# A scan layer and a routed transformer layer in one kernel: where the first batch's router scores are computed, and how the pools of the two layers are cut

## The chip, the cores and the metric

The kernel runs on one core of one Trainium2 chip. The metric is the time of one execution in microseconds (us) of device time. Three executions of the kernel before took 4037.52, 4037.91 and 4040.02 us; the median is 4037.91 us. One execution was taken by the profiler: it took 4038.12 us and its trace spans 4036.3 us from the first to the last instruction.

## The reference, cut to what matters

x is 16 batches of 1024 tokens of 512 float32 numbers. Layer 0 is a selective scan (16 states per channel) with a residual; layer 1 is a routed transformer layer: a router scores every token, the best 127 tokens of a batch go through attention and a feed-forward network, the others pass.

```python
# layer 0
x = x + s6(layernorm(x), A_log, D, x_proj_w, dt_proj_w, dt_proj_b)
#   s6: delta = softplus(...); h = exp(delta*A)*h + delta*B*u over the tokens; y = sum(h*C) + u*D
# layer 1, on h = layernorm(x) of the result
weights = (h @ router_w)[..., 0] + router_b[0]      # one score per token
topv, topi = top_k(weights, 128); thr = topv[:, -1]
sel_idx = sort(topi[:, :127])
x_sel, pos_sel, w_sel, m_sel = h, positions, weights and mask rows at sel_idx
x1 = x_sel + attention(rmsnorm(x_sel, ln1), m_sel) @ wo
x2 = x1 + gelu(rmsnorm(x1, ln2) @ w1) @ w2
out = put x2 * w_sel at sel_idx, plus h where weight <= thr
x = x + out
```

## The kernel before, in words

**The scan** (`scan_layer`) works through 32 halves: 16 batches, two halves of 512 tokens each. A half is 64 steps g: 16 states n by 4 channel blocks dc of 128 channels. For one step TensorE builds the input db in one of four PSUM banks of 2 KB (`turn`, lines 308 to 321, two steps ahead), ScalarE builds the decay da (`decays`, five steps ahead) and the scaled input v (`scaled`, eight ahead), VectorE does the recurrence in place (`recur`, line 329), GpSimd multiplies two steps' result by C (`weighed`, line 341) and TensorE sums the states into y (`summed`, line 360, six steps behind). SyncE's queue fetches dg twelve steps ahead (`diagonals`, line 283) and ct (`fetch`). While one half runs, the small generators `prep` (softplus and input of the next half) and `stats` (mean and variance of the next batch) are advanced one piece per step by `until(k)`. `finish` (line 249) turns y back and adds it to x1 in device memory by a GpSimd-issued DMA (line 265). The last half has no `prep` and no `stats` beside it.

**The routed layer** (`ffn_layer`) is a software pipeline of periods p of 28 ticks each. In period p these generators are advanced tick by tick, in this order: `feed(p-1)`, `attention(p)`, `keep_others(p)`, `select(p+1)`, `scores(p+2)`. So period -2 has scores(0) alone, period -1 has select(0) and scores(1), period 0 has attention(0), select(1), scores(2), and so on.
- `scores(b)` (lines 618 to 660): for each of 8 chunks of 128 tokens, VectorE takes bn_stats and bn_aggr of x1 and a product with the router's weight row rw, summed (lines 630, 631, 633); then 1/sqrt(variance) and the score of every token; the scores go through a TensorE transpose (652), a DMA to device memory (656) and a DMA that broadcasts them to 128 partitions, w_row (658).
- `select(b)` ranks each token's score against the whole row: three VectorE counts for each chunk (676, 680, 685; the last one needs the triangular matrix `earlier`), the one-hot sel (696), a matmul (710), two gathers by GpSimd (726, 730), and at last the normalized input hnT of the attention.

**Order.** Within each layer's `manual_schedule` block, the instructions of an engine keep the order in which the generators issue them. Instructions outside these blocks, such as the constants and weight loads ahead of the routed layer's loop, are placed by the scheduler: in the trace, VectorE runs line 568 (ahead of the block) after line 630 (inside it).

**Memory.** Pools of SBUF are stacked. The scan's are `s_const` (2 KB and less for each tile), `s_pool` (all large tiles: xt, u, uT, delta, rest, du, dg, v, da, hc, ct, yT) and `s_small`. At the end of `scan_layer` they are given back, and the routed layer's `f_const`, `f_keep`, `f_row`, `f_small` take the same addresses. `f_const` holds the projections wq, wk, wv, wo (1 MB each) and w1, w2 (4 MB each), loaded by twelve DMAs on ScalarE's queue (lines 552, 556, 558).

The loop that sets which generators run:

```python
for p in range(-2, B + 1):
    stages = [stage(b) for stage, b in ((feed, p - 1), (attention, p), (keep_others, p),
              (select, p + 1), (scores, p + 2)) if 0 <= b < B]
    for k in range(PERIOD):
        clock[0] = k
        ...
        for g in list(stages):
            if next(g, "end") == "end": stages.remove(g)
```

Of the kernel before, what the change touches and what calls it, by code (L numbers as in the profile page):

```python
# [19 lines left out]
P = 128  # L20
# [11 lines left out]

@with_exitstack
def scan_layer(ctx, tc, x, x1_dram, a_log, dskip, xpT, dtT, dtb, ident):
# [27 lines left out]
    const = ctx.enter_context(tc.tile_pool(name="s_const", bufs=1))  # L62
    pool = ctx.enter_context(tc.tile_pool(name="s_pool", bufs=2))
    small = ctx.enter_context(tc.tile_pool(name="s_small", bufs=2))
# [24 lines left out]
    eye = const.tile([P, S], F32, tag="eye", name="eye")  # L89
# [3 lines left out]
    skip = const.tile([P, ND, S], F32, tag="skip", name="skip")  # L93
# [155 lines left out]
    def finish(b, half, ys, over):  # L249

        s = f"{b}_{half}"
        turned = over.rearrange("p c (j i r) -> p c j i r", i=NS, r=S)
        yield from until(BEHIND + 1)
        yT = []
        for i in range(NS):
            yT.append(pool.tile([P, LH], F32, tag="yT", bufs=4, name=f"yT_{s}_{i}"))
            nc.scalar.copy(yT[i], ys[i])
        for i in range(NS):
# [7 lines left out]
            x1_dram[b][:, half * TH : (half + 1) * TH, :], over, accum_op=ALU.add  # L266
        )
# [32 lines left out]
    def decays(g):  # L300
        h, n, dc = at(g)
        if dc == 0:
            da_of[h, n] = pool.tile([P, ND, LH], F32, tag="da", bufs=4, name=f"da_{h}_{n}")
        nc.scalar.activation(  # L304
            da_of[h, n][:, dc, :], live[h][1][:, dc, :], AF.Exp, scale=a_sb[:, dc, n : n + 1]
        )
# [27 lines left out]
    def weighed(g):  # L334
# [5 lines left out]
        hc = pool.tile([P, 2, LH], F32, tag="hc", bufs=6, name=f"hc_{h}_{n}_{dc}")  # L340
# [10 lines left out]
    def fetch(h, n):  # L351
        t = pool.tile([P, G, LH], F32, tag="ct", bufs=4, name=f"ct_{h}_{n}")
        nc.sync.dma_start(t, rows_c[h][n : n + G, :].partition_broadcast(P))
        ct_next[h, n] = t
# [28 lines left out]
    with tc.manual_schedule():  # L383
# [10 lines left out]
        for g in range(-AHEAD_D, total + per_half // 2):  # L394
# [4 lines left out]
            if g % per_half == 0 and 0 <= g <= total:  # L399
                h = g // per_half  # L400
                if h + 1 < len(halves):
                    running.append(prep(*halves[h + 1]))
            if 0 <= g + AHEAD_D < total:
                diagonals(g + AHEAD_D)
# [26 lines left out]
            if k >= 0 and k % per_half == per_half - 1 and k < total:  # L431
                h = k // per_half
                running.append(finish(*halves[h], ys_of.pop(h), live.pop(h)[2]))
# [7 lines left out]
def ffn_layer(  # L441
    ctx, tc, x1_dram, mask, pos, router_w, router_b, wq, wk, wv, wo, w1, w2, ln1, ln2, out, ident
# [22 lines left out]
    const = ctx.enter_context(tc.tile_pool(name="f_const", bufs=1))  # L465
    keep = ctx.enter_context(tc.tile_pool(name="f_keep", bufs=2))
    row = ctx.enter_context(tc.tile_pool(name="f_row", bufs=2))
    small = ctx.enter_context(tc.tile_pool(name="f_small", bufs=3))
    dram = ctx.enter_context(tc.tile_pool(name="f_dram", bufs=2, space=DRAM))
# [18 lines left out]
    for q in (0, 2, 4):  # L488
        load(0, q, "x1a")
    rw = const.tile([P, D], F32, tag="rw", name="rw")  # L490
    nc.sync.dma_start(rw, router_w.rearrange("d o -> (o d)").partition_broadcast(P))
    rb = const.tile([P, 1], F32, tag="rb", name="rb")
    nc.sync.dma_start(rb, router_b.partition_broadcast(P))

    gains = const.tile([ND, 2, P], F32, tag="gains", name="gains")
    for i, g in enumerate((ln1, ln2)):
        nc.sync.dma_start(gains[:, i, :], g.rearrange("(c p) -> c p", p=P))
# [10 lines left out]
    )  # L508
    inv = const.tile([P, HH], F32, tag="inv", name="inv")
# [3 lines left out]
    for i in range(HH):  # L513
        nc.vector.memset(inv[:, i : i + 1], float(freq[i]))

    pos_i = const.tile([MB * NT, P], I32, tag="pos_i", name="pos_i")
    for m in range(MB):
        nc.sync.dma_start(
            pos_i[m * NT : (m + 1) * NT, :], pos[m, 0:L].rearrange("(c p) -> c p", p=P)
        )  # L520
    pos_r = const.tile([MB * NT, P], F32, tag="pos_r", name="pos_r")
    nc.vector.tensor_copy(pos_r, pos_i)
    pos_ps = pst.tile([P, 512], F32, tag="tp", name="pos_ps")
    nc.tensor.transpose(pos_ps[:, : MB * NT], pos_r, ident[: MB * NT, : MB * NT])
    pos_f = const.tile([P, MB, NT], F32, tag="pos_f", name="pos_f")
    nc.vector.tensor_copy(pos_f.rearrange("p m c -> p (m c)"), pos_ps[:, : MB * NT])


    POS, WT, TOK, ROW, RSTD, OFF, SIDE = range(7)
    sides = []  # L530
    for i in range(3):
        t = const.tile([P, NT, SIDE], F32, tag=f"side{i}", name=f"side{i}")
        nc.gpsimd.iota(
            t[:, :, TOK], pattern=[[P, NT]], base=0, channel_multiplier=1,
            allow_small_or_imprecise_dtypes=True,
        )
        nc.gpsimd.iota(
            t[:, :, ROW], pattern=[[1, NT]], base=0, channel_multiplier=NT,
            allow_small_or_imprecise_dtypes=True,
        )  # L540
        sides.append(t)

    w_pad = []
    for i in range(2):
        t = const.tile([P, P], F32, tag=f"w_pad{i}", name=f"w_pad{i}")
        nc.vector.memset(t, 0.0)
        w_pad.append(t)

    proj = {}
    for name, wt in (("wq", wq), ("wk", wk), ("wv", wv), ("wo", wo)):  # L550
        proj[name] = const.tile([P, ND, D], F32, tag=name, name=f"{name}_sb")
        nc.scalar.dma_start(proj[name], wt.rearrange("(c p) e -> p c e", p=P))
    w1_sb = const.tile([P, ND, F], F32, tag="w1", name="w1_sb")
    w2_sb = const.tile([P, NF, D], F32, tag="w2", name="w2_sb")
    for c in range(ND):
        nc.scalar.dma_start(w1_sb[:, c, :], w1[c * P : (c + 1) * P, :])
    for c in range(0, NF, ND):
        nc.scalar.dma_start(
            w2_sb[:, c : c + ND, :],
            w2[c * P : (c + ND) * P, :].rearrange("(c p) e -> p c e", p=P),  # L560
        )
    gain = const.tile([P, 2, ND], F32, tag="gain", name="gain")
    for i in range(2):
        g_ps = pst.tile([P, 512], F32, tag="tp", name=f"g_ps{i}")
        nc.tensor.transpose(g_ps[:, :ND], gains[:, i, :], ident[:ND, :ND])
        nc.vector.tensor_copy(gain[:, i, :], g_ps[:, :ND])
    rw_sum = const.tile([P, 1], F32, tag="rw_sum", name="rw_sum")
    nc.vector.tensor_reduce(rw_sum, rw, AX.X, ALU.add)
# [9 lines left out]
    w_row_of, keeping, picked, attended = {}, {}, {}, {}  # L578
# [12 lines left out]
    def taken(ps, name, tag, bufs=1):  # L591
        t = row.tile(list(ps.shape), F32, tag=tag, bufs=bufs, name=name)
# [3 lines left out]
    def gained(ps, i, name, tag):  # L596

        t = row.tile([P, ND, P], F32, tag=tag, bufs=1, name=name)
# [19 lines left out]
    def scores(b):  # L618

        side, wp = sides[b % 3], w_pad[b % 2]  # L620
        w_col = wp[:, :NT]
        st = small.tile([P, NT, nc.vector.BN_STATS_DIM], F32, tag="st", name=f"st_{b}")
        mv = small.tile([P, NT, nc.vector.BN_AGGR_DIM], F32, tag="mv", name=f"mv_{b}")
        xd = small.tile([P, NT], F32, tag="xd", name=f"xd_{b}")
# [410 lines left out]
```

## Time and profile before

| stretch of the profiled execution | us | what |
|---|---|---|
| whole execution / span of its trace | 4038.12 / 4036.3 | |
| 2722.25 to 2807.36 | 85.11 | half 30 of the scan, with the last `prep` beside it |
| 2807.36 to 2882.42 | 75.06 | half 31, the last, with nothing beside it |
| 2882.42 to 2904.00 | 21.58 | last products of GpSimd, `finish`, the DMA that adds y to x1 |
| 2904.00 to 2951.03 | 47.03 | period -2: constants, weights, scores(0) |
| 2951.03 to 2993.64 | 42.61 | period -1: select(0), scores(1) |
| 2993.64 to 3056.92 | 63.28 | period 0 |
| 3056.92 to 3119.03 | 62.11 | period 1; the later ones take about 62 us as well |

The stretches begin and end with VectorE's first or last instruction of the stage. How to read the profile: a timeline row gives start, duration, engine, line, operation, out<-in and count, and in brackets how long the engine had been idle and what ended that. Busy times of VectorE's instructions overlap a little, so a start-to-start distance is shorter than the recorded duration. A window row gives each engine's busy time in a stretch, the clock that TensorE was granted, and the share of time that the 16 DMA engines were busy.

### The profile page before, as it was taken

How to read it: one execution, taken by the hardware profiler on the slowest of the kernel's cores; microseconds unless marked ns; L12 is line 12 of the kernel's file. 1: busy time of each engine (PE TensorE's matmuls, PEld its weight loads, DVE VectorE, ACT ScalarE, POOL GpSimd, SP SyncE). 2: the span in 40 equal slices, each digit the busy share in tenths (PEclk: the TensorE clock that was granted, in tenths of full speed). 3: DMA queues.
4: the chain of work that ended last, by engine and by line, in shares of the span. 5: the costliest groups of instructions: out<-in, count | busy, mean ns of one | idle time of the engine just before them, and what ended most of it. 6: DMA issues, size and time to landing. Idle time of an engine off the chain costs nothing.

```text
span 4036.3 us, 89081 instructions
## 1 busy us (share of the span) xinstructions
PE 3607.3 (89%) x35349; PEld 2272.0 (56%) x35349; DVE 3439.1 (85%) x5142; ACT 3169.2 (79%) x5525; POOL 2716.9 (67%) x1454
## 2 busy tenths in 40 slices
PE   6999999998999999999999999899638999999996
PEld 4666666655666665566666656566324555555453
DVE  5999999999999999999999999999666776867741
ACT  6999999999999999999999999999415455455552
POOL 4899999988999998899999889999600111010110
PEclk8999999999999999999999999999758999999998
DMA  5343433434343343434344343433453434434331
GB/s 152 88 121 82 121 102 103 110 99 122 85 121 95 107 106 106 120 83 121 82 120 111 100 122 86 117 85 104 126 190 106 146 92 154 128 110 150 109 92 33
DMA packets 367466, 444.48 MB, mean 110 GB/s; under 512 B 182381, under 2 KB 252185, under 8 KB 362442
## 3 DMA queue, kind: packets, MB, share of 16 engines
q1 hardware_dynamic: 317080, 371.32, 30.4%
q0 software_dynamic: 40960, 50.55, 6.6%
q10 hardware_dynamic: 9010, 16.91, 1.1%
q8 instruction: 279, 4.57, 0.5%
q14 instruction: 137, 1.12, 0.1%
HBM read 361.36 MB, written 110.66 MB: 117 GB/s over the span
## 4 chain that ended last, share of the span: by engine, by line
PE 44%; DVE 36%; ACT 10%; issue 5%; DMA 3%; POOL 1%; POOLq 0%; DVEq 0%; ACTq 0%; SPq 0%
DVE da L329 19%; PE db L316 13%; PE y L360 8%; PE db L318 6%; PE ff_ps L939 4%; ACT da L304 4%; PE pp L176 3%; ACT v L296 2%; DVE junk L680 2%; DVE junk L676 2%; PE tpy L262 2%; DVE st L630 1%; PE at_ps L896 1%; DVE xw L633 1%; PE tpu L169 1%
## 5 line engine op out<-in xcount | busy, mean ns | idle before, releaser
L341 POOL TENSOR_TENSOR hc<-da,ct 128x1024 f32<-128x1024 f32 x1024 | 2410.5, 2389 | 250.3 <-DVE da L329 193.2
L304 ACT ACTIVATE da<-delta,a_sb 128x512 f32<-128x512 f32 x2048 | 1403.5, 712 | 33.5 <-POOL carry L347 28.5
L316 PE MATMUL db<-dg,du 128*128 128x128 f32 x7168 | 1262.9, 293 | 149.4 <-DVE da L329 130.8
L316 PEld LDWEIGHTS db<-dg,du 128*128 128x128 f32 x7168 | 970.7, 191 | 718.3 <-DVE da L329 542.4
L329 DVE TENSOR_TENSOR_SCAN da<-da,carry,db 128x512 f32<-128x512 f32 x1024 | 1227.7, 1258 | 59.3 <-PE db L318 59.3
L329 DVE TENSOR_TENSOR_SCAN da<-da,db 128x512 f32<-128x512 f32 x1024 | 1175.3, 1197 | 75.1 <-PE db L318 55.3
L318 PE MATMUL db<-ident,v 128*128 128x128 f32 x4608 | 842.1, 274 | 0.0
L296 ACT ACTIVATE v<-du,bT 128x512 f32<-128x512 f32 x1152 | 822.6, 714 | 11.8 <-DVE du L247 6.2
L360 PE MATMUL y<-hc,eye 32*32 32x512 f32 x16384 | 633.0, 606 | 3.2 <-POOL hc L341 2.9
L318 PEld LDWEIGHTS db<-ident,v 128*128 128x128 f32 x4608 | 577.0, 143 | 0.0
L705 POOL PARTITION_ALL_REDUCE thr<-thr_s x16 | 6.2, 385 | 488.0 <-DVE thr_s L704 488.0
L946 POOL DMA_INDIRECT out<-xs,at x16 | 76.0, 4748 | 360.9 <-DVE trig L779 263.0
L939 PE MATMUL ff_ps<-w_sb,gT 128*128 128x512 f32 x512 | 278.3, 663 | 0.0
L914 PE MATMUL up<-w_sb,h2T 128*128 128x512 f32 x512 | 240.5, 598 | 4.0 <-DVE h2T L599 4.0
L360 PEld LDWEIGHTS y<-hc,eye 32*32 32x32 f32 x16384 | 141.0, 103 | 128.9 <-issue 87.2
L208 PE MATMUL z<-xp,dt_sb 97*128 97x512 f32 x256 | 141.6, 636 | 45.1 <-DVE da L329 43.2
L233 POOL TENSOR_TENSOR delta<-delta,rest 128x1024 f32<-128x1024 f32 x64 | 152.0, 2375 | 31.9 <-ACT delta L230 31.9
L593 ACT COPY gT<-tp_g 128x512 f32<-128x512 f32 x64 | 38.2, 596 | 165.6 <-PE tp_g L588 165.6
L914 PEld LDWEIGHTS up<-w_sb,h2T 128*128 128x128 f32 x512 | 92.7, 191 | 100.5 <-issue 92.6
L863 ACT ACTIVATE a<-a,mx 128x127 f32<-128x127 f32 x256 | 98.8, 387 | 54.5 <-DVE mx L861 52.1
L680 DVE TENSOR_SCALAR_CACHE_REDUCE junk<-w_row,side 128x1024 bf16<-128x1024 f32 (+7 forms) x128 | 103.4, 808 | 44.6 <-DMA w_row<-w_dram 44.6
L939 PEld LDWEIGHTS ff_ps<-w_sb,gT 128*128 128x128 f32 x512 | 95.3, 209 | 65.6 <-issue 65.5
(191 smaller groups left out, 3961.2 us busy)
## 6 DMA issues: line engine op xcount, KB each, us to landing
ct<-bc SPq DMA_DIRECT2D x256, 512.0 KB
dg<-field SPq DMA_DIRECT2D x384, 128.0 KB
xt<-in_x SPq DMA_DIRECT2D x32, 1024.0 KB
x<-in_x SPq DMA_DIRECT2D x16, 2048.0 KB
x<-du POOLq DMA_DIRECT2D x32, 1024.0 KB, 8.0
x1a<-x SPq DMA_DIRECT2D x64, 512.0 KB
x1b<-x SPq DMA_DIRECT2D x64, 512.0 KB
out<-x1b SPq DMA_DIRECT2D x64, 512.0 KB
```

Of the source, the lines that this page charges most:

```text
L208: nc.tensor.matmul(z, dt_sb[:, dc * P : (dc + 1) * P], xp, start=True, stop=True)
L233: nc.gpsimd.tensor_tensor(delta[:, dc : dc + 2, :], delta[:, dc : dc + 2, :], rest[:, dc : dc + 2, :], ALU.add)
L296: nc.scalar.activation(v_of[h, n][:, c - m, :], du[:, c, :], AF.Copy, scale=bT[:, c, n : n + 1])
L304: nc.scalar.activation(da_of[h, n][:, dc, :], live[h][1][:, dc, :], AF.Exp, scale=a_sb[:, dc, n : n + 1])
L316: nc.tensor.matmul(out, live[h][2][:, c, ch], dg[:, c, :], start=True, stop=True)
L318: nc.tensor.transpose(out, v[:, c - m, ch], ident)
L329: nc.vector.tensor_tensor_scan(da[:, dc, :], da[:, dc, :], db_of.pop(g), carry[b][:, dc, n : n + 1] if half else 0.0, ALU.mult, ALU.add,)
L341: nc.gpsimd.tensor_tensor(hc, da_of[h, n][:, dc - 1 : dc + 1, :], ct_of[h][:, n % G, :].unsqueeze(1).to_broadcast([P, 2, LH]), ALU.mult,)
L360: nc.tensor.matmul(ys[i][j * S : (j + 1) * S, :], weights(r, j), rows(r, j), start=start, stop=stop, tile_position=(i * S, j * S),)
L680: nc.vector.tensor_scalar(junk[:, lo:], w_row[:, lo:], mine, None, ALU.is_gt, ALU.add, accum_out=cnt[:, 1, c : c + 1],)
L914: nc.tensor.matmul(up, h2T[:, c, :], w1_sb[:, c, f * 512 : (f + 1) * 512], start=(c == 0), stop=(c == ND - 1),)
L939: nc.tensor.matmul(ff_ps, gT[f][:, c, :], w2_sb[:, f * 4 + c, :], start=(f == 0 and c == 0), stop=(f == UP - 1 and c == 3),)
```

## The change

- A class `Router` takes over the router's constants, the side tables, the score buffers and `scores`. It is built ahead of the scan, so its tiles (w_row among them) lie below both layers' pools.
- In the scan's last half a new generator `first_scores` runs where `prep` would. At step 1 it issues the constants' DMAs (rw, rb, two gains, four positions) and loads x1 of batch 0 (four DMAs of 512 KB) into the tile that held xt. At step 8 it prepares the constants. Then for each chunk c a matmul with the identity copies x1 into a PSUM bank at step 9 + 4c, and at step 10 + 4c VectorE does the three score instructions on that bank. At steps 42, 44 and 46 follow 1/sqrt(variance), here as Ln and Exp on ScalarE, the scores, and their way to w_row.
- The routed layer starts with period -1. There scores(1) runs its chunks at ticks 9 to 16 instead of 0 to 5, 13 and 14.
- The scan's pools: da, hc, ct, yT, eye and skip move to a new pool `s_last`, stacked last; the last half's `finish` writes into a da buffer instead of du. The routed layer's pools are stacked as `f_small`, `f_keep`, `f_row`, `f_const` (now without w1, w2), then `f_late` (the tags first written at tick 24 of period -1 or later) and `f_heavy` (w1, w2).
- The projections are loaded on SyncE's queue, alternating with the loads of x1 of batch 1. w1 and w2 are loaded in eight pieces of 1 MB on SyncE's queue at ticks 1 to 8 of period 0. The 16 small writes of `inv` move into select(0).

```diff
+    def scores(self, b, until, slots, chunk, scratch, bank, root, ahead=0):
...
+        for c in range(NT):
+            yield from until(slots[c] - ahead)
+            x1 = chunk(c)
+            yield from until(slots[c])
+            nc.vector.bn_stats(st[:, c, :], x1)
+            nc.vector.bn_aggr(mv[:, c, :], st[:, c, :])
+            nc.vector.scalar_tensor_tensor(
+                scratch(c), x1, 1.0, self.rw, ALU.mult, ALU.mult, accum_out=xd[:, c : c + 1]
+            )
+        yield from until(slots[NT])
...
+            nc.scalar.activation(var, mv[:, :, 1], AF.Ln, bias=self.eps)
+            nc.scalar.activation(rstd, var, AF.Exp, scale=-0.5)
+            yield from until(slots[NT + 1])
+        nc.vector.scalar_tensor_tensor(off, mv[:, :, 0], -1.0, rstd, ALU.mult, ALU.mult)
+
+        nc.vector.tensor_tensor(xd, xd, rstd, ALU.mult)
+        nc.vector.scalar_tensor_tensor(xd, off, self.rw_sum, xd, ALU.mult, ALU.add)
+        nc.vector.tensor_scalar(w_col, xd, self.rb, None, ALU.add)
+        nc.vector.tensor_copy(side[:, :, self.WT], w_col)
+        nc.vector.tensor_copy(side[:, :, self.POS], self.pos_f[:, min(b, self.MB - 1), :])
...
@@ scan_layer
     const = ctx.enter_context(tc.tile_pool(name="s_const", bufs=1))
+    small = ctx.enter_context(tc.tile_pool(name="s_small", bufs=2))
     pool = ctx.enter_context(tc.tile_pool(name="s_pool", bufs=2))
-    small = ctx.enter_context(tc.tile_pool(name="s_small", bufs=2))
+
+    last = ctx.enter_context(tc.tile_pool(name="s_last", bufs=2))
...
+        if over is None:
+            over = last.tile([P, TH, D], F32, tag="da", bufs=4, name="over_last")
...
+    def first_scores():
+
+        yield from until(1)
+        constants = router.constants(bank)
+        next(constants)
+        x1 = pool.tile([P, NT, D], F32, tag="xt", bufs=1, name="x1_early")
+        for q in range(0, NT, 2):
+            nc.sync.dma_start(x1[:, q : q + 2, :], x1_dram[0][:, q : q + 2, :])
+        yield from until(8)
+        _drain(constants)
+        junk = pool.tile([P, TH, D], F32, tag="u", bufs=1, name="junk_early")
+
+        def lifted(c):
+
+            t = bank(f"lift_{c}")
+            nc.tensor.matmul(t, ident, x1[:, c, :], start=True, stop=True)
+            return t
+
+        yield from router.scores(
+            0, until, [10 + 4 * c for c in range(NT)] + [42, 44, 46], lifted,
+            lambda c: junk[:, c % TH, :], bank, False, 1,
+        )
...
                 if h + 1 < len(halves):
                     running.append(prep(*halves[h + 1]))
+                elif h < len(halves):
+                    running.append(first_scores())
...
@@ ffn_layer
-    const = ctx.enter_context(tc.tile_pool(name="f_const", bufs=1))
+    small = ctx.enter_context(tc.tile_pool(name="f_small", bufs=3))
     keep = ctx.enter_context(tc.tile_pool(name="f_keep", bufs=2))
     row = ctx.enter_context(tc.tile_pool(name="f_row", bufs=2))
-    small = ctx.enter_context(tc.tile_pool(name="f_small", bufs=3))
-    dram = ctx.enter_context(tc.tile_pool(name="f_dram", bufs=2, space=DRAM))
+    const = ctx.enter_context(tc.tile_pool(name="f_const", bufs=1))
+
+    late = ctx.enter_context(tc.tile_pool(name="f_late", bufs=2))
+    heavy = ctx.enter_context(tc.tile_pool(name="f_heavy", bufs=1))
...
+    for q, (name, wt) in enumerate((("wq", wq), ("wk", wk), ("wv", wv), ("wo", wo))):
+        if q < 3:
+            load(1, 2 * q, "x1a")
+        nc.sync.dma_start(proj[name], wt.rearrange("(c p) e -> p c e", p=P))
...
+    def load_heavy(i):
+        if i < ND:
+            nc.sync.dma_start(w1_sb[:, i, :], w1[i * P : (i + 1) * P, :])
...
+        first = 9 if b == 1 else 0
...
     with tc.manual_schedule():
-        for p in range(-2, B + 1):
+        for p in range(-1, B + 1):
...
+                if p == 0 and 1 <= k <= ND + NF // ND:
+                    load_heavy(k - 1)
```

## The prediction

> **What bounds the kernel now.** I read the chain that ended last first. Up to 2882 us it alternates between VectorE's recurrences, TensorE and GpSimd; then, for some 70 us, it is a string of waits and transfers (columns: start us, us, what):
>
> ```profile
> 2888.59 7.23 issue
> 2895.84 7.79 DMA x<-du
> 2904.26 13.87 DMA wk_sb<-in_wk
> 2919.10 4.69 DMA pos_i<-in_pos
> ...
> 2928.47 8.90 DMA x1a<-x
> 2937.39 0.74 ACTq L558
> 2938.17 1.28 ACT L640
> 2941.58 4.33 DMA w_dram<-w_t
> 2945.93 4.97 DMA w_row<-w_dram
> 2951.03 1.29 DVE junk L680 x2
> ```
>
> Every engine starts the routed layer only after the scan's last DMA, x<-du, has landed (2904), and select(0)'s first count waits until 2951 for scores(0). Busy times by stretch come second (stretch, length, then PE, PEld, DVE, ACT, POOL busy, clock, DMA share, GB/s):
>
> ```profile
> 2807.36:2882.42 75.06, 73.38 (x914) 47.23 (x914) 75.06 (x65) 58.30 (x95) 75.06 (x36) 1.00 0.26 69
> 2882.42:2904.00 21.58, 10.14 (x78) 4.01 (x76) 0.03 (x1) 4.30 (x8) 7.05 (x4) 0.50 0.28 50
> 2904.00:2951.00 47.00, 1.08 (x4) 0.64 (x4) 14.14 (x65) 1.75 (x3) 0.99 (x8) 0.50 0.96 363
> 2951.00:2993.60 42.60, 12.59 (x49) 10.23 (x50) 30.91 (x120) 9.30 (x20) 2.65 (x3) 0.54 0.39 126
> ```
>
> In the last half VectorE has no idle time at all, so work added there lengthens it. For the 68.6 us behind it (2882.42 to 2951.03) VectorE does only 14.2 us of work. Third, what a VectorE instruction costs beside GpSimd's products, from the groups by line of VectorE (busy us, mean ns):
>
> ```profile
> L138 DVE BATCH_NORM_STATS2 st<-xt 128x6 f32<-128x512 f32 x128 | 86.6, 676 | 3.1 <-DMA xt<-in_x 3.1
> L213 DVE SCALAR_TENSOR_TENSOR rest<-z,delta 128x512 f32<-128x512 f32 x128 | 86.0, 672 | 18.6 <-ACT delta L211 18.5
> L633 DVE SCALAR_TENSOR_TENSOR xw<-x1a,rw 128x512 f32<-128x512 f32 x128 | 84.2, 658 | 0.0
> L146 DVE SCALAR_TENSOR_TENSOR off<-mv,rstd 128x8 f32<-128x8 f32 x16 | 9.1, 570 | 2.1 <-ACT rstd L144 1.9
> ```
>
> The first two run in the scan at the speed of the third, which runs with GpSimd idle. The fourth, 8 elements wide, takes 570 ns where its twin at line 643 takes 174; its two inputs are both SBUF tiles. The timelines around one of them show why (VectorE, then GpSimd):
>
> ```profile
> 2609.67 0.63 DVE L146 SCALAR_TENSOR_TENSOR off<-mv,rstd 128x8 f32<-128x8 f32 x1
> 2610.22 3.43 DVE L329 TENSOR_TENSOR_SCAN da<-da,db 128x512 f32<-128x512 f32 x3
> ```
> ```profile
> 2607.91 2.36 POOL L341 TENSOR_TENSOR hc<-da,ct 128x1024 f32<-128x1024 f32 x1
> 2610.24 2.37 POOL L233 TENSOR_TENSOR delta<-delta,rest 128x1024 f32<-128x1024 f32 x1
> ```
>
> It ends when GpSimd's running product ends.
>
> **The sum.** The profiled execution took 4038.1 us, 0.2 above the median of 4037.9; the sum is made on it.
>
> (a) *scores(0) in the last half.* For eight chunks: bn_stats, bn_aggr and product follow each other every 1.41 us in period -2 (2926.95 to 2928.36): 11.3 us. No row has bn_stats on a PSUM bank; line 213, which reads one, is 14 ns from line 633, which doesn't, so I take the same; bounds 10.5 and, at 0.3 us more for each of 16 reads, 16. Constants: two memsets 0.31, cast 0.2, the round trip by TensorE 0.54 (pos_r's end to pos_f), copies 0.14, the reduction 0.6: 1.9 with the eps. Tail: 1.0 (2939.94 to 2940.95), plus 0.8 for waiting on GpSimd's products (about 0.5 at line 146, a little for the constants). All 15.0 is on the path, since nothing there is idle. And waits can come with it: half 29, of the same kind as half 31 but with `prep` beside it, took 87.15 by VectorE's timeline (2635.10 to 2722.25), 12.1 more, for twelve VectorE instructions of 0.62 start to start, 7.5; 4.6 are waits, most of them of recurrences for db. Here TensorE gets eight matmuls of 512 columns, as from `prep`, but not its 36 transposes; I add 1.0. Together **16.0**; bounds 12.5 (the instructions alone, cheap) and 21.
>
> Hidden beside it: TensorE's eight copies at 0.43 (wq_ps: 1.72 for four), 3.4 us, since weight loads wait for VectorE's banks (32.9 us between 2700 and 2880); 4 us if that cover is gone. ScalarE's Ln and Exp with two table loads of 1.28: it is busy 58.3 of 75.06. GpSimd's six iotas, 0.14 each: with 15 us more for the same 32 products it gets idle time. SyncE issues twelve more DMAs, about 0.37 each (line 486), 4.4 us, and 2 MB at the 0.4 MB/us of period -2 is 5.2: 9.6 us in which dg behind them can be late, against 10 steps of 1.17 between dg's issue and its use. It just fits; a few us if it doesn't. The wait for w_t at step 46 holds the last dg's, with 8 steps in hand.
>
> (b) *The gap.* VectorE's last recurrence is at 2882.4 + 16.0 = 2898.4; call it T. The tiles in `s_pool` and below (by their sizes 112 KB a partition, against 98 for `f_small` to `f_const`) are last read by TensorE's last db, before T. So select(0) may start at T, w_row having been there for 17 steps. **Removed: 68.6.** What is late next is `earlier`: its affine_select (0.29) sits on GpSimd, whose last product runs from T to T + 2.4, and the third count would start at T + 1.3: **+1.4**; bounds 0 and, if GpSimd's queue puts it behind x<-du (`finish` issues that 7.25 after the last product), +9.8. `finish` itself leaves the path: x<-du lands at about T + 18, and `f_late` is first written at T + 35.
>
> Loads: four projections and 1.5 MB of x1 now start at T - 3, 5.5 MB, 14 us, done by T + 11; wq is first read at T + 35. If that cover were gone, 14 us at most.
>
> (c) *Period -1 took 42.6.* Six chunks of scores(1) no longer stand between select's counts: -8.5. Three of them, ticks 9 to 11, now stand ahead of the gathers, beside the 2.2 us for which VectorE waited on line 714: +2.0. The other five and 1.9 us of angles run beside the gathers (7.9 us), and the variance, 9 us behind them, then holds ScalarE's xs by about 0.8; the Sqrt table load (1.28), formerly done in period -2, comes in ahead of it: together +1.8. **-4.7**, bounds -8 (TensorE granted more than 0.54 after a shorter pause) and -2.
>
> (d) *Period 0 and later.* w1 and w2 were loaded in period -2; now 8 MB, 21 us, are issued from tick 1, done by about 25 us into a period of 63; first read at its end. SyncE's x1 loads and stores queue behind them, for chunks needed 30 us later. 0, bounds -1 and +5. The `inv` writes, 0.37, lie in a wait for the gathers. Later periods have the same instructions: 0.
>
> Sum: 4038.1 + 16.0 - 68.6 + 1.4 - 4.7 = **3982**.
>
> **A page against the trace.** The rule beside line 146 is in the Trainium skill, GPSIMD Engine Reference, Key points: GpSimd shares its SBUF interfaces with VectorE, and contends with instructions that have two SBUF inputs or run in a 2-port mode. By the trace line 146 agrees (570 against 174 ns). By that page the tail's scaling, copies and the constants' memsets, which no row shows beside a product, could wait too; that is rival 3.
>
> **Rivals.**
> 1. *GpSimd does x<-du first.* `earlier` comes at T + 11.1, the counts stand still: 8.4 more, **3991**. For it: before, the iotas followed x<-du (2904.32). Against: then no address was free earlier, and the scheduler does reorder such instructions.
> 2. *The pools are not split in effect*: some tile of the first four still waits for x<-du's landing, T + 17.8. The counts start 16.5 later than in the sum: **3999**. For it: before, even `f_keep` waited so. Against: the sizes above.
> 3. *Small VectorE instructions in the last half wait for whole products.* Ten of them (three memsets, the cast, three two-input ones of the tail, its scaling, two copies) at 2.36, less the 0.8 counted: up to +22, at half of it **3993**. Against: GpSimd has a product to run only when VectorE has finished a pair of recurrences, so one wait empties its queue.
> 4. *The other side: the chunks' instructions wait as well.* 24 and the ten above at 2.36 are 80 us instead of 16: 3982 + 64 = **4046**. It decides from 56 / 2.36 = 24 whole waits on. Against: lines 138 and 213 run beside products at full speed.
>
> **Chances.** Sum as worked out 0.62; rival 1 0.14; rival 2 0.08; rival 3 0.10; rival 4 0.05; a little is left for a wait I don't see. Range 3970 (the low bounds of a, b, c) to 4003 (rival 2 with most of a's bound). 0.2% is 8 us, about what a measurement of this kernel can tell from no change; all but rival 4 lie far beyond it: faster 0.94, same 0.01, slower 0.05.
>
> **What would show it.** In the changed kernel: half 31 near 91 us with VectorE hardly idle and the chunk's instructions at 0.67 to 0.7; the first count within 3 us of the last recurrence; `earlier` ahead of x<-du on GpSimd; the projections' DMAs issued before the last product; w_row for select(1) some 38 us after the first count; period 0 at 63. It would be wrong if VectorE showed idle time in the last half for dg or banks, if any early tile of the routed layer waited for x<-du, or if feed(0) waited for w1.

## The result and the profile after

The changed kernel takes 3997.72 us (median of four runs, 3996.20 to 3998.99) against 4038.55 for the kernel before beside it: a ratio of 0.9896, with a 95% interval of 0.9881 to 0.9912. The forecast was 3982, with 3970 to 4003 around it: the right side and inside the range, but only 41 of the 56 us came. The profiled execution took 3996.66 us, its span is 3994.9.

The stretches, cut as for the kernel before (by VectorE's first or last instruction of the stage):

| stretch | before, us | after, us | difference | forecast |
|---|---|---|---|---|
| up to the last half | 2807.36 | 2805.87 | -1.5 | 0 |
| half 31 | 75.06 | 101.25 | +26.2 | +16.0 |
| from the last recurrence to select(0)'s first count | 68.62 | 0.06 | -68.6 | -68.6 |
| period -1, with its wait for `earlier` | 42.61 | 42.81 | +0.2 | +1.4 - 4.7 |
| period 0 | 63.28 | 63.63 | +0.35 | 0 |
| the rest | 979.32 | 981.27 | +1.95 | 0 |

The first row and the last two are no effect of the change that can be told apart: among the kernels below, whose code there is the same or nearly so, the first half alone varies from 91.9 to 93.9 us, period 0 from 60.9 to 63.6, and the rest from 976.3 to 981.3.

The same three windows as before, of the changed kernel (stretch, length, then PE, PEld, DVE, ACT, POOL busy, clock, DMA share, GB/s), half 31, period -1 and period 0:

```profile
2805.87:2907.12 101.25, 82.88 (x962) 52.60 (x962) 95.07 (x112) 61.55 (x100) 80.18 (x43) 0.93 0.29 90
2907.12:2949.99 42.87, 19.68 (x98) 14.17 (x99) 31.25 (x138) 15.52 (x29) 6.52 (x8) 0.62 0.83 268
2949.99:3013.63 63.64, 39.88 (x170) 25.29 (x169) 44.80 (x149) 23.12 (x63) 2.33 (x3) 0.64 0.67 246
```

In half 31 VectorE's busy time is 6.2 short of the length (it was equal to it before), and the busy time has grown by 20, not by 15. The stretch of 21.58 us that ended with the DMA x<-du, and the 47 of period -2, are gone. So is their string of transfers in the chain that ended last (start us, us, what):

```profile
2904.70 2.43 DVE da L478 x2
2907.47 2.31 POOL hc L490
...
2921.97 1.67 DVE sel L777 x8
...
2928.93 6.86 DMA m_rows<-in_mask,at
2935.84 1.98 PE tp_m L700 x8
...
2943.11 2.07 DMA w_dram<-w_t
2945.20 4.68 DMA w_row<-w_dram
```

The recurrences run straight into the counts, by way of one product of GpSimd. Where half 31 grew by more than the sum said stands in VectorE's timeline at step 8, where the constants are prepared:

```profile
2816.61 5.42 DVE L89 CAST pos_r<-pos_i 32x128 f32<-32x128 int32 x1
2822.50 0.19 DVE L93 COPY pos_f<-pos_ps 128x32 f32<-128x32 f32 x1 [0.47 <-PE pos_ps L91]
...
2829.64 0.70 DVE L118 BATCH_NORM_STATS2 r_st<-lift 128x6 f32<-128x512 f32 x1 [3.83 <-PE lift L410]
```

The same cast in the kernel before, where GpSimd was idle:

```profile
2923.91 0.21 DVE L522 CAST pos_r<-pos_i 32x128 f32<-32x128 int32 x1 [4.17 <-DMA pos_i<-in_pos]
```

GpSimd and TensorE beside the cast of the changed kernel:

```profile
2814.89 7.07 POOL L490 TENSOR_TENSOR hc<-da,ct 128x1024 f32<-128x1024 f32 x3
2824.86 2.35 POOL L490 TENSOR_TENSOR hc<-da,ct 128x1024 f32<-128x1024 f32 x1 [2.91 <-DVE da L478]
```
```profile
2822.18 0.28 PE L91 MATMUL pos_ps<-ident,pos_r 32*128 32x32 f32 x1 [6.74 <-DVE pos_r L89]
```

The cast of 32 x 128 numbers, put at 0.2 us, takes 5.42: it ends as the third of three products in a row ends (2821.96). TensorE, which keeps its order, stands for 6.74 us behind the transpose of pos_r, and is then late with the first copy of x1: VectorE waits 3.83 us for it, and 0.69 and 0.81 for the next two, 5.3 in all (2.3 of them are there without the cast too, as a kernel below shows). The chunks' instructions themselves cost what was forecast. By the groups of VectorE in half 31 (busy us, mean ns of one, idle before them):

```profile
L118 DVE BATCH_NORM_STATS2 r_st<-lift 128x6 f32<-128x512 f32 x8 | 5.5, 683 | 5.3 <-PE lift L410 5.3
L120 DVE SCALAR_TENSOR_TENSOR junk_early<-lift,rw 128x512 f32<-128x512 f32 x8 | 5.3, 658 | 0.0
L135 DVE SCALAR_TENSOR_TENSOR side<-r_mv,side 128x8 f32<-128x8 f32 x1 | 1.5, 1456 | 0.0
```

### The profile page after: what moved, and what is told of

Read it like the earlier page. It is cut to its first block, busy times and chain, and to the rows that moved or that the text cites. A ratio compares the mean times of both kernels' runs of the same rounds, so it can differ in the third digit from the quotient of the medians.

```text
span 3994.9 us, 89107 instructions
## 1 busy us (share of the span) xinstructions
PE 3607.0 (90%) x35365; PEld 2273.8 (57%) x35365; DVE 3445.5 (86%) x5140; ACT 3172.6 (79%) x5528; POOL 2717.0 (68%) x1454
## 4 chain that ended last, share of the span: by engine, by line
PE 43%; DVE 38%; ACT 11%; issue 5%; DMA 3%; POOL 0%; POOLq 0%; DVEq 0%; ACTq 0%; SPq 0%
DVE da L478 20%; PE db L465 12%; PE y L509 8%; PE db L467 6%; PE ff_ps L1023 4%; ACT da L453 4%; PE pp L300 3%; ACT v L445 3%; DVE junk L761 2%; DVE junk L757 2%; DVE r_st L118 2%; PE tpy L388 2%; PE at_ps L980 1%; DVE xw L120 1%; PE tpu L293 1%
## 5 line engine op out<-in xcount | busy, mean ns | idle before, releaser
L509 PE MATMUL y<-hc,eye 32*32 32x512 f32 x16384 | 620.8, 603 | 2.6 <-POOL hc L490 2.6
```

Source lines behind the costliest of these rows:

```text
L509: nc.tensor.matmul(ys[i][j * S : (j + 1) * S, :], weights(r, j), rows(r, j), start=start, stop=stop, tile_position=(i * S, j * S),)
```

## The experiments

In the main comparisons theory A is the reading above, and theory B a rival that each run names. Medians are of four runs beside seven of the kernel before, if nothing else is said; ratios are to that kernel, with 95% intervals.

**The changed kernel once more.**

> The changed kernel once more, on the chip of v3_thr_pe and v4_later: 3996 to 3999 if that chip is as the first; v3_thr_pe is 14 to 17 us and v4_later 15 to 19 us faster than it.

3994.69 us (3993.21 to 3995.32) against 4039.79: 0.9891 [0.9874, 0.9907]. Half 31 is 100.88, its cast 5.36, period -1 42.92. The cast and the waits are read as in the first execution; VectorE's wait for the first copy is 2.83 here. The gain over this run of the two kernels `v3_thr_pe` and `v4_later` below was expected at 14 to 17 and 15 to 19 us; their medians are 5.8 and 7.1 below it.

**The cast by ScalarE.**

```diff
-        nc.vector.tensor_copy(pos_r, pos_i)
+        nc.scalar.copy(pos_r, pos_i)
```

> The integer positions are converted by ScalarE instead of VectorE; nothing else differs from the changed kernel. Theory A (the cast waits for GpSimd's products, and TensorE, queued behind it, then brings db and the first copies late): the last half falls from 101.25 us by 5.2 for the cast and by most of the 5.3 of idle time ahead of bn_stats, to about 91; the kernel from 3998 to 3987 or 3988. Theory B (the idle time comes from x1's loads and from the copies' banks): only the cast's 5.2 go, the last half is 96, the kernel 3992 or 3993.

3991.52 us (3988.51 to 3991.78) against 4040.80: 0.9874 [0.9858, 0.9891]. Half 31 of that kernel, and VectorE's longest wait in it:

```profile
2809.41:2902.50 93.09, 79.67 (x962) 50.33 (x962) 89.68 (x111) 61.71 (x101) 80.15 (x43) 1.00 0.33 98
```
```profile
2825.01 0.70 DVE L118 BATCH_NORM_STATS2 r_st<-lift 128x6 f32<-128x512 f32 x1 [1.29 <-PE lift L410]
```

One instruction on another engine takes 8.2 us out of the half: the cast's 5.4, and 2.8 of waits. The three waits for the copies fall from 5.3 to 2.8 in all, so about half of them came from the cast; the half lies between the two theories (91 and 96).

**The constants later.** They are prepared ahead of the last copy, at step 37, when GpSimd has no backlog.

```diff
-        yield from until(8)
-        _drain(constants)
...
         def lifted(c):
+            if c == NT - 1:
+                _drain(constants)
             t = bank(f"lift_{c}")
```

> The constants' second part (cast on VectorE, its transposes, copies, the reduction) moves from step 8 to step 37, ahead of the last copy, where GpSimd has no products waiting. Theory A (the cast waits until GpSimd's backlog is empty, which at step 8 is three products): it takes at most one running product, 0.2 to 2.4 us, instead of 5.4, TensorE is held for no longer; the last half is 93 to 97 us. Theory B (this cast beside GpSimd always costs about 5, and TensorE behind it as much again): the last half stays at 100 to 102.

3986.38 us (3984.51 to 3988.72) against 4037.66: 0.9872 [0.9856, 0.9889]; half 31 is 94.26. The same cast on the same engine, which came 0.3 us before GpSimd's running product ended:

```profile
2865.06 0.36 DVE L89 CAST pos_r<-pos_i 32x128 f32<-32x128 int32 x1
```

**The constants earlier.** All of them are prepared ahead of the first half, when GpSimd has no product yet.

```diff
         load(0)
+        constants = router.constants(bank)
+        next(constants)
         clock[0] = per_half
         _drain(stats(0))
+        _drain(constants)
...
-        constants = router.constants(bank)
-        next(constants)
         x1 = pool.tile([P, NT, D], F32, tag="xt", bufs=1, name="x1_early")
...
-        yield from until(8)
-        _drain(constants)
```

> All of the router's constants are prepared ahead of the scan's first half, where VectorE waits anyway. Theory A (the constants, not the chunks, made the last half 10 us longer than forecast): the last half is 89 to 91.5 us, the kernel 10 to 11.5 faster than the changed one, 3 less than that if the scan's start is put off by the additional loads. Theory B (the chunks' copies by TensorE start late whatever stands ahead of them): 94 to 97, and 4 to 7 faster.

3984.76 us (3981.13 to 3988.05) against 4037.66: 0.9865 [0.9849, 0.9882]. Half 31:

```profile
2809.53:2901.01 91.48, 80.14 (x959) 51.51 (x959) 88.66 (x105) 61.62 (x100) 79.63 (x37) 0.98 0.31 94
```

This is 9.8 us less, and near the 91 that the prediction gave to the half. But that 91 held 1.9 us for the constants, which are done elsewhere here, so some 2.3 us that it had missed remain. Of the idle time three waits for copies are left, 0.84, 0.69 and 0.81: 2.3 in all, where 1.0 had been put.

**What waits for GpSimd, by itself.** To the last kernel sixteen instructions are added on VectorE that nothing waits for, from SBUF to SBUF: the cast again, and a plain float32 copy of the same size, by turns.

```diff
+    def probe():
+        for i, k in enumerate((4, 6, 8, 10, 12, 16, 20, 24, 28, 32, 36, 40, 44, 48, 52, 56)):
+            yield from until(k)
+            if i % 2 == 0:
+                nc.vector.tensor_copy(router.pos_r, router.pos_i)
+            else:
+                nc.vector.tensor_copy(router.pos_r, router.rw[: router.MB * router.NT, :P])
```

> The kernel with all of the router's constants ahead of the first half, and sixteen added instructions on VectorE in the last half that nothing waits for: eight casts of the positions (32 x 128, int32 to float32, SBUF to SBUF) ahead of steps 4, 8, 12, 20, 28, 36, 44 and 52, and eight plain float32 copies of the same size between them, at 6, 10, 16, 24, 32, 40, 48 and 56. It measures the disputed cost by itself. Theory A: the cast waits for GpSimd because it takes part in the sharing of SBUF, and then the plain copy, also SBUF to SBUF, does too. Of 91 us GpSimd is busy for some 80, with products of 2.36; an instruction that comes at any time waits on average half a product, so both kinds are expected at a mean of 0.2 + 0.9 x 1.2 = 1.3 us, spread from 0.2 to 2.6, and more only where two or three products stand in a row and none lets it in (the 5.4 us of the changed kernel). The half grows from 91.5 by 16 x 1.3 = 21, to about 112. Theory B: it is the conversion alone that waits; the copies take 0.15 to 0.25 each, the casts 1.3, and the half is near 104. Theory C: the 5.4 us were something of that one place; all sixteen take 0.2 to 0.4 and the half is near 96. Whether the wait ends with the running product or only when no product is left is read from the casts that come during the first of several products in a row.

One run: 4007.32 against 4034.39. Half 31 is 113.3 us, 21.8 more than without the sixteen. VectorE, the first four and one of the later ones, then GpSimd:

```profile
2813.51 0.34 DVE L400 CAST pos_r<-pos_i 32x128 f32<-32x128 int32 x1
...
2816.14 4.79 DVE L402 COPY pos_r<-rw 32x128 f32<-32x128 f32 x1
...
2823.21 1.48 DVE L400 CAST pos_r<-pos_i 32x128 f32<-32x128 int32 x1
...
2830.35 0.21 DVE L402 COPY pos_r<-rw 32x128 f32<-32x128 f32 x1
...
2840.40 1.52 DVE L402 COPY pos_r<-rw 32x128 f32<-32x128 f32 x1
```
```profile
2813.86 6.99 POOL L495 TENSOR_TENSOR hc<-da,ct 128x1024 f32<-128x1024 f32 x3
2822.26 2.35 POOL L495 TENSOR_TENSOR hc<-da,ct 128x1024 f32<-128x1024 f32 x1 [1.41 <-DVE da L483]
...
2839.48 2.36 POOL L495 TENSOR_TENSOR hc<-da,ct 128x1024 f32<-128x1024 f32 x1 [1.42 <-DVE da L483]
```

So the wait is not one of the conversion: the plain copy waits as well. Twelve of the sixteen took 1.45 to 1.54, to the end of the product that was running (2822.26 + 2.35 is 2824.61, the cast ends at 2824.69); three took 0.21 to 0.34, as a product ended or with none running. And one, a plain copy, came 0.1 us before the end of the first of three products in a row and waited for the other two as well: 4.79 us. The cast of the changed kernel came 0.7 us before the end of the first of its three, and was let in at neither of the two boundaries.

**x1 read from SBUF, without the copies into PSUM.**

```diff
-            t = bank(f"lift_{c}")
-            nc.tensor.matmul(t, ident, x1[:, c, :], start=True, stop=True)
-            return t
+            return x1[:, c, :]
```

In the changed kernel:

> The scores in the last half read x1 straight from SBUF; the eight copies by TensorE are left out. Theory A (an instruction with two SBUF inputs waits for GpSimd's running product): the eight products x1 * rw take 1.1 to 2.9 us each instead of 0.58, bn_stats stays at 0.7; the last half grows by 4 to 16 us, the kernel to 4002 to 4014. Theory B (the wait of line 146 in the kernel before is a matter of very small instructions, or hidden): the products stay at 0.6, the kernel is at 3996 to 3998.

3996.95 us (3991.82 to 3999.19) against 4040.80: 0.9886 [0.9869, 0.9902]; half 31 is 101.14, as with the copies. The group of the eight products, and one of them beside GpSimd's products:

```profile
L120 DVE SCALAR_TENSOR_TENSOR junk_early<-x_early,rw 128x512 f32<-128x512 f32 x8 | 10.4, 1297 | 0.0
```
```profile
2857.77 1.17 DVE L120 SCALAR_TENSOR_TENSOR junk_early<-x_early,rw 128x512 f32<-128x512 f32 x1
```
```profile
2853.69 4.71 POOL L488 TENSOR_TENSOR hc<-da,ct 128x1024 f32<-128x1024 f32 x2 [1.90 <-DVE da L476]
```

The product with two SBUF inputs takes 1297 ns instead of 658, 5.1 us for eight, and the wait of VectorE for late copies, 5.3, is gone: no net effect. Nothing else of the chunk waits; bn_stats, with one SBUF input and 6 elements out, took 0.66 while GpSimd's product ran. Where the copies are less late (2.3 us of waits in all), that is with all constants ahead of the scan (the kernel `v2_all_first` below), the same edit costs more than it saves:

> As v2_all_first, but x1 is read from SBUF and the copies by TensorE are left out. Theory A (each product waits 0.6 for the end of GpSimd's running one, while the copies cost next to nothing once the cast is out of the way): 3 to 5 us slower than v2_all_first. Theory B (TensorE, at 1.16 us a step against VectorE's 1.17, has no room for the copies, so that they cost what they save): within 1 us of it.

3987.52 us (3986.81 to 3992.57) against 4037.66: 0.9878 [0.9862, 0.9895], 3.5 us above that kernel in the medians, with overlapping intervals. In the traces half 31 is 97.75 against 91.56, and a product takes 1716 ns on average:

```profile
L131 DVE SCALAR_TENSOR_TENSOR junk_early<-x_early,rw 128x512 f32<-128x512 f32 x8 | 13.7, 1716 | 0.0
```

But that average is of unlike cases. The first product came while GpSimd had five of its own in a row, and took 4.75; the other seven took 1.06 to 2.05, 1.28 on average, as in the run above.

```profile
2822.26 4.75 DVE L131 SCALAR_TENSOR_TENSOR junk_early<-x_early,rw 128x512 f32<-128x512 f32 x1
```
```profile
2814.73 11.73 POOL L495 TENSOR_TENSOR hc<-da,ct 128x1024 f32<-128x1024 f32 x5
```

It came in the fourth of the five (2821.72 to 2824.17) and ended 0.5 us after the fifth: this instruction too, with two SBUF inputs, was not let in at the boundary. So the copies by TensorE are worth about 6 us of the half there, 4.1 of them by that one product, and nothing in the kernel as it was changed.

**One pool for the scan's large tiles**, the rest as changed.

```diff
-    last = ctx.enter_context(tc.tile_pool(name="s_last", bufs=2))
+    last = pool
```

> The tiles of s_last go back into s_pool; all else is as in the changed kernel. Theory A (the first four pools of the routed layer would wait for x<-du to land): the first count starts 17 to 18 us after the last recurrence instead of 0.1, the wait for the triangular matrix (1.7) goes, and the gathers, no longer beside x<-du, are 2 us quicker: the kernel takes 4011 to 4014. Theory B (select(0) would be held by something else that late anyway): 3998 to 4002.

4014.00 us (4010.76 to 4015.43) against 4040.80: 0.9931 [0.9914, 0.9947]. GpSimd's timeline, from x<-du's issue to `earlier`:

```profile
2920.99 0.88 POOL L391 DMA_DIRECT2D x<-over_last  x1 [7.18 <-ACT over_last L390]
2929.45 0.23 POOL L647 IOTA slot_no<- 128x128 f32 x1 [7.58 <-DMA x<-over_last]
2929.65 0.28 POOL L653 TENSOR_SCALAR_AFFINE_SELECT earlier<-earlier 128x128 f32<-128x128 f32 x1
```

The first count starts 17.94 us after the last recurrence (rival 2 had 17.8), when that DMA has landed. Period -1 takes 40.43 there instead of 42.81, so the split is worth some 14 to 16 us by the ratios (0.0035 and 0.0040 of 4038 against the two measurements of the changed kernel).

**The pools and the loads as changed, scores(0) behind the scan.** The loop starts with period -2 again, whose x1 is loaded with the projections; the router's constants are prepared there too (not shown below).

```diff
-                elif h < len(halves):
-                    running.append(first_scores())
...
-            load(1, 2 * q, "x1a")
+            load(0, 2 * q, "x1a")
...
-        first = 9 if b == 1 else 0
+        first = 0
...
-        for p in range(-1, B + 1):
+        for p in range(-2, B + 1):
```

> Pools and weight loads as changed, but scores(0) and the router's constants stay behind the scan in a period -2, reading x1 from SBUF with GpSimd idle. The last half is 75 us again (26.2 less). Theory A (period -2 was long because of the weights' transfers on its queues and of its late start): it takes 28 to 36 us from the last recurrence on, and period -1 is 39 to 43; the kernel takes 4000 to 4008, so that moving the scores is worth 2 to 10 us and pools with loads the rest of the 41. Theory B (period -2 stays at 47): 4018 or so, and the move is worth 20.

4001.25 us (4000.57 to 4004.54) against 4040.80: 0.9900 [0.9884, 0.9917]. The last half and the stretch up to the first count:

```profile
2810.68:2885.73 75.05, 73.35 (x914) 47.20 (x914) 75.05 (x66) 58.30 (x95) 75.05 (x36) 1.00 0.29 79
2885.73:2915.20 29.47, 10.25 (x82) 4.41 (x80) 14.02 (x45) 6.05 (x11) 7.88 (x6) 0.59 0.86 296
```

and the chain in it:

```profile
2885.76 4.06 DMA x1a<-x
...
2894.03 8.59 DMA x1a<-x
...
2907.82 3.70 DMA w_dram<-w_t
2911.53 3.53 DMA w_row<-w_dram
```

Of the 68.6 us, 39.1 go by the pools and the loads alone, without a score in the scan. The other 29.5 are what scores(0) takes behind the scan, and it takes 26.2 within it: its move, as it was made, gained 3 us of these, and 0.9896 and 0.9900 can't be told apart.

**Towards a faster kernel.** With all constants ahead of the first half, `slot_no` and `earlier` too:

```diff
+        self.slot_no = const.tile([P, P], F32, tag="slot_no", name="slot_no")
...
+        self.earlier = earlier = const.tile([P, P], F32, tag="earlier", name="earlier")
+        nc.vector.memset(earlier, 1.0)
...
-    slot_no = const.tile([P, P], F32, tag="slot_no", name="slot_no")
...
+    slot_no, earlier = router.slot_no, router.earlier
```

> As v1_const_first, and slot_no and the triangular matrix are prepared there too. Theory A (the third count waits only for the triangular matrix behind GpSimd's last product): the 1.7 us of wait at the first chunk go, and the kernel is 1.5 to 2 faster than v1_const_first. Theory B (the count, which has two SBUF inputs, then waits for GpSimd's running product in place of the matrix): 0 to 0.7 faster.

3984.05 us (3978.88 to 3987.11) against 4037.66: 0.9863 [0.9847, 0.9879]. The 1.7 us of waiting for `earlier` went, but period -1 is 42.96 us against 43.05. The third count, which waited for `earlier` before, now waits for GpSimd's last product in the other way, as an instruction with two SBUF inputs (it takes 0.35 elsewhere):

```profile
2900.53 1.54 DVE L766 SCALAR_TENSOR_TENSOR tie<-w_row,side,earlier 128x128 f32<-128x128 f32 x1
```

Period -1 took 41.1 us without its wait for `earlier`, where 37.9 were forecast. In the changed kernel x<-du (there named x<-over_last) is the last thing issued ahead of the gathers, since it stands on GpSimd's queue behind the threshold's all-reduce:

```profile
2924.17 0.41 POOL L786 PARTITION_ALL_REDUCE thr<-thr_s  x1 [14.15 <-DVE thr_s L785]
2924.46 1.06 POOL L391 DMA_DIRECT2D x<-over_last  x1
2928.93 1.12 POOL L807 DMA_INDIRECT m_rows<-in_mask,at  x1 [3.41 <-DVE rest L817]
```

From the gather's issue to its use by TensorE it is 6.9 us, against 4.8 in the kernel before. In the next kernel the sum over the partitions for batch 0 is made by TensorE, so that nothing holds x<-du:

```diff
-        nc.gpsimd.partition_all_reduce(thr, thr_s, P, bass_isa.ReduceOp.add)
+        if b == 0:
+            thr_ps = pst.tile([P, 512], F32, tag="tp", name="thr_ps")
+            nc.tensor.matmul(thr_ps[:, :1], router.ones, thr_s, start=True, stop=True)
+            nc.scalar.copy(thr, thr_ps[:, :1])
+        else:
+            nc.gpsimd.partition_all_reduce(thr, thr_s, P, bass_isa.ReduceOp.add)
```

> As v2_all_first, but the threshold of batch 0 is summed over the partitions by a matmul with ones instead of GpSimd's all-reduce, so nothing of select(0) stands ahead of x<-du on GpSimd. Theory A (the gathers of period -1 are slow because x<-du is issued just ahead of them, on the same queue): x<-du is issued 9 to 10 us after the last recurrence instead of 17, the first gather lands 4.5 to 5.2 us after its issue instead of 7.1, period -1 falls from 43.0 to 40.5 to 41.5, the kernel is 1.5 to 2.5 faster than v2_all_first. Theory B (the loads of x1 and of the weights slow the gathers): period -1 stays at 42.5 to 43.5.

3988.88 us (3985.13 to 3990.24) against 4039.79: 0.9878 [0.9862, 0.9895]. The order is as meant:

```profile
2909.14 0.88 POOL L404 DMA_DIRECT2D x<-over_last  x1 [7.15 <-ACT over_last L403]
2921.54 1.12 POOL L814 DMA_INDIRECT m_rows<-in_mask,at  x1 [11.52 <-DMA x1a<-x]
```

The gather takes 4.9 us to its use, 2.0 less than in the changed kernel. But period -1 is 42.55, 0.4 less than in `v2_all_first`: from the issue of w_dram to that of w_row it now takes 3.1 us instead of 2.1 (1.2 in the kernel before), and the rest went in small parts. No gain shows in the whole either: 0.9878 against 0.9863, where 1.5 to 2.5 us less were expected. At last w1 and w2 start three ticks later, in case they are what slows w_row, and the row's DMAs are issued at step 49 instead of 46, in case they hold dg:

```diff
-                if p == 0 and 1 <= k <= ND + NF // ND:
-                    load_heavy(k - 1)
+                if p == 0 and 4 <= k <= 3 + ND + NF // ND:
+                    load_heavy(k - 4)
...
-... + [42, 44, 46], lifted
+... + [42, 44, 49], lifted
```

> As v3_thr_pe, with w1 and w2 loaded at ticks 4 to 11 of period 0 instead of 1 to 8, and the scores' transpose in the last half at step 49 instead of 46. Theory A (select(1)'s w_row lands late, 4.6 to 4.8 us after its issue against 3.9 before the change, because the first piece of w1 is issued right behind it; and TensorE, held by the transpose, is what makes VectorE wait 1.1 us at step 57): w_row lands in 3.6 to 4.0, the wait at step 57 goes, and the kernel is 1.5 to 2.5 faster than v3_thr_pe. Theory B (neither): the same within 0.5.

3987.58 us (3983.15 to 3990.78) against 4039.79: 0.9877 [0.9860, 0.9893]. VectorE's wait of 1.1 us late in the half is gone (half 31 is 91.31). Period -1 is 42.11. From w_row's issue to the first count it is still 4.87 us, against 4.80 in the changed kernel and 3.91 in the one before, so w1 alone is not the cause. It does not clear transfers in general: with w1 moved, the store of `out` is issued 0.4 us behind w_row, where nothing followed it for 1.8 us in the kernel before. What slows these two transfers of batch 1 (4 KB, and 512 KB written) was not settled.

## Why the prediction was right in its sign and 16 us short

*(a), half 31, +16.0: a term mis-sized, +26.2.* The chunks came as worked out: 11.2 of VectorE's time against 11.3, and bn_stats reads a PSUM bank at 683 ns where 676 were expected. The tail with the wait of `off` took 2.2 against some 1.5. The term that failed is "cast 0.2", with "a little for the constants" in the 0.8 for waiting on GpSimd: the cast took 5.4. The second is the 1.0 for other waits: those for the copies took 5.3, of which 2.3 are there without the cast as well, so TensorE's standstill behind the cast made 3.0 (2.0 in the second execution, whose first wait was 2.83). Moving that cast alone to another engine gave 8.2 back, and taking the constants out of the half 9.8. Rival 3 had the mechanism ("small VectorE instructions wait for whole products") with the wrong reason against it ("one wait empties its queue"): that holds in the middle of the half, where the probes took 1.5, but at step 8 GpSimd has three products to run, and one wait lasts for all three. 0.8 us, a third of a product, was put in for ten instructions; one of them waited for more than two.

By the Trainium skill (VectorE: DVE Perf Modes, What auto-detection actually checks), a one-source instruction with source and destination in SBUF can take a 2-port mode on further conditions; in such a mode, by GPSIMD Engine Reference, Key points, it contends with GpSimd. The trace agrees: cast and plain copy waited, 1.5 us in twelve of sixteen cases, and the products that read x1 from PSUM stayed at 658 ns, where those with two SBUF inputs took 1297 on average. By its page SBUF — State Buffer (SBUF: two separate sides) whichever of the two starts first has the shared ports for its whole instruction; twelve of the sixteen cases agree, but where three products stood in a row the waiting cast did not get its turn at the next boundary. The prediction had the second page, but did not ask which of its ten small instructions stands where GpSimd has a backlog.

*(b), the gap, -68.6 and `earlier` +1.4: right.* It is 68.56 us, and the wait for `earlier` 1.71. GpSimd did put x<-du behind it, so rival 1 did not occur; the pools are split in effect, and with one pool the counts start 17.94 after the last recurrence, so rival 2 was priced about right (17 us above the sum; 14 to 16 by the ratios).

*(c), period -1, -4.7: too much, -1.5.* The order of the counts and gathers was read rightly: the gathers were issued 21.75 us after the first count, where 26.55 before, less 8.5, plus 2.0 and the 1.4 of `earlier` make 21.45. What was left out are transfers. x<-du, no longer on the chain, is now issued ahead of the gathers on the same queue, and they take 2.1 longer to their use. Behind them the period grew by 2.9, where +1.8 stood: 1.2 up to the first DMA of w_row, and 0.9 for each of its two DMAs, which the sum did not have. Their rows before:

```profile
2988.51 1.21 DMA w_dram<-w_t
2989.74 3.79 DMA w_row<-w_dram
```

The gathers' share was shown by moving x<-du (4.9 instead of 6.9). The cause of the other is open, and it took the gain back when the gathers were faster. In the second execution of the changed kernel the first of the two DMAs took 1.2, as before the change, and the gathers 7.5.

*(d), period 0 and later, 0: right*, within what the same code varies by (63.6 against 63.3, other runs 60.9 to 63.6).

*Rival 4, the other side*, did not occur: it needed 24 whole waits, and the chunks' bn_stats and products took 0.68 and 0.66 on the PSUM banks, beside GpSimd's products, as lines 138 and 213 had in the trace of before.

Of the whole change, the pools and loads give nearly all that it gained: 0.9900 without the scores in the scan, 0.9896 with them, and 0.9865 or 0.9863 with the scores in the scan and the constants out of its last half: by these ratios 10 to 13 us faster than the kernel as changed. The two kernels built on these, measured directly beside it, are 5.8 and 7.1 faster in the medians; half 31 is 8 to 10 us shorter in all four.

*The range.* The 26.2 of (a) is beyond its own upper bound of 21, and (c) beyond -2. That 3998 still fell inside the range is in part luck: the upper end was set by rival 2, a delay that did not occur. The lower end, 3970, is some 4 below what the low bounds of (a), (b) and (c) add up to: 4038.1 + 12.5 - 68.6 + 0 - 8 = 3974.

## What to carry to other kernels

When work is moved to where VectorE has no idle time, cost not only its instructions but ask of each, also the smallest, whether it is a copy, a cast or has two inputs in SBUF while GpSimd is busy, how many instructions GpSimd has ready at that place, and what stands behind it in the in-order engines: one cast of 0.2 us cost 8 here. Setup that depends on nothing belongs where the other engines are still empty, not where there is room in the schedule of the engine that needs it. A transfer that leaves the chain is still in a queue: look for what it now stands ahead of.

## What the runs showed of the hardware that was not expected

- A VectorE copy or cast from SBUF to SBUF that came while GpSimd had several products ready waited for all of them, not only for the running one: 5.35 to 5.42 us for the cast in four profiled executions with three products in a row and 4.79 for a copy, against 1.45 to 1.54 with one product left and 0.21 to 0.36 with none in the way. In the changed kernel the recurrence that feeds the third product had ended at 2815.5, before the cast began at 2816.61.
- It is no rule without exception. In the run with the constants at step 37 the cast did get in between two products that followed each other closely (0.36 us); the input of the second came 0.1 us after the cast had begun. And line 146 of the kernel before, 8 elements with two SBUF inputs, came in a running product in 15 of its 16 cases, with the next following at once, and took 0.45 to 0.65: it ended with the running product. In the case that the prediction shows, the next is line 233's, whose input ScalarE had finished at 2606.8. What tells these cases from the 4.75 us of the product with two SBUF inputs, no run shows.
- The wait hits a plain float32 copy just as the conversion from int32. It does not hit all that reads or writes SBUF: beside GpSimd's products two memsets of 128 x 128 took 0.31 together (the same as with GpSimd idle), bn_stats from SBUF 0.66, and the first count, from SBUF to SBUF with an accumulator, 1.25 in `v2_all_first` (1.28 with GpSimd idle).
- From the issue of batch 1's w_dram to that of w_row, 1.2 us passed in the kernel before and with scores(0) behind the scan, where the last loads of x1 had been issued 7.4 us ahead, and 2.0 to 3.1 in all other kernels, where they had been issued 3 to 5 us ahead (but 1.2 in the second execution of the changed kernel, with 4.9). That points at these loads; no run moved them. w_row, 3.9 before, took 4.6 to 5.1 in every changed kernel.
